# Second attention: features of q by head, on 64-row halves of the partitions, and scores in one pass

## The chip, the cores and the metric

The kernel runs on one core of one Trainium2 chip. The metric is the device time of one execution in microseconds (us), as the median of several executions. A profile of one further execution goes with it: its span, its engines (PE for matmuls, PEld for the loading of weights, DVE, ACT, POOL, and SP, which only issues DMAs here), and every instruction with its start and duration.

## What is computed

The program is two layers on an input of 4 batches of 512 tokens by 128 features. Each layer normalises x, computes an attention s and a gated mixture of experts g, and adds s * silu(g) to x. The change concerns the attention of the second layer, 16 heads of 8 dimensions, repeated over 16 "wavelength" channels:

```
Q, K, V = x Wq + bq, x Wk + bk, x Wv + bv     # per head: [512, 8]
for each channel w:   m = cos(phase[w, head])
    scores = (Q m)(K m)^T / sqrt(8);  scores *= cos(KERR scores^2)
    acc += softmax(scores) V * interference_weight[w]
out = (acc / 16) Wo + bo
```

With the data's sizes the inner cosine is 1, and the channel only scales the scores by a number a between 0 and 1. The kernel therefore does not compute 16 softmaxes. It writes exp(a s) as a sum of six functions of s: exp(A s), its square and its cube, and s squared, s and 1. The first three ("bank 0") need the scores of all pairs of query and key; the last three ("bank 1") need only sums over the keys of products of the components of k and v, and then a product with features of q. A numerator and a denominator of each channel are then mixtures of the banks. If the data were outside the assumed sizes, a second, general version of the program would run after it; it does not run here.

## The kernel before

The last stage of the program, `attn1`, is a loop of 64 steps i = 0 to 63: for each of the 4 batches b, 16 steps t = 0 to 15; step t works on the group m = t // 4 of four heads and on the block t % 4 of 128 keys. Instructions that go through the helpers `mm1` (L318), `act1` (L321), `vec1`, `pool1` and `dma1` (L330) keep the order in which they are written, on each engine, so the order within a step is the order of the text.

A step issues, on PE, the scores of the *next* step (`scores1`; the page calls the tile `s`), then the sums over keys of *this* step (`over_keys`; tile `acc`). ACT computes exp(A s) of the next step and then its square, in two halves of 128x1024 each (`function1`), and DVE the cube as the product of the two (L1548). `acc` of a step takes the three functions one after the other; the cube comes last. Every fourth step begins a new group of heads: there DVE first copies `acc` away (L1590, tile `bank`), and the next `acc` has to wait for that copy.

The scores are exact to about 24 bits although they are bf16 matmuls: q and k are split into three bf16 parts each (`partq`, `partk`), and 8 products of parts per dimension are summed. A head has 8 dimensions times 8 products, 64 rows. Before the change these lie as two sets x = 0, 1 of 32 rows; four heads stand beside each other on the 128 partitions; `scores1` (L1525) runs two passes of four matmuls of 32 rows, the second of which adds to the first.

Bank 1 of group m is two matmuls in `bank1` (L1328), one of 65 rows (`rows1`: 32 components of q of four heads, their squares, a row of ones) and one of 128 rows (`rows2`: the products of component d with component d + 1 to d + 4 of the same head, cyclically). Their weights `lin` come from `forms` (L1272): sums over the 4 blocks of 128 tokens of products of `feat` (the same features of k, made on POOL at L1203 to L1218) with v; only the diagonal blocks, where the head of the feature is the head of v, are kept by the multiplication with `count` (L1286, L1290). `features1` (L1312) fetches the rows of q from DRAM by 6 DMAs per group (`qe`, `qd`) into `rows1`, `rows2` and a buffer `other`, and POOL multiplies (L1324, L1325).

Extra work is placed on the steps by hand. `mixing` (L1593) gives the steps at which `bank1`, `sums1` (denominators), `quotients1` and `output1` run, and `prepare1` (L1168) spreads the preparation of the next batch over steps 0 to 15 by a table (tokens 0, 1 and 13, projections 2 and 3, `forms` 5, 7, 10 and 11). At steps with t % 4 = 0 this extra PE work stands ahead of `acc`, at the others behind it. The preparation of batch 0 runs between the experts of the stage before (`prepare`). PSUM tiles with the tag "mix", two buffers, are shared by `bank1`, `sums1`, `quotients1` and `output1`. `end1` finishes the last batch.

## Time and profile before

| | us |
|---|---|
| median of 3 runs (lowest, highest) | 886.55 (886.23, 888.0) |
| profiled execution | 890.56 |
| its span, first to last instruction | 888.8 |
| PE, DVE, ACT, POOL busy in the span | 850.0, 596.3, 520.1, 383.4 |
| loop of the second attention in the span | about 534 to 868 |
| end of the last batch | about 868 to 888.8 |

An fp32 matmul stands in the trace as two matmuls, each with its weight load, so `x4` of the tile `b` is one call of `bank1`. Tiles of matmuls are written rows*columns of the array ("65*128"). Matmuls in different tiles of the array run beside each other, so the busy time of a group is less than the number of its instructions times the duration of one. The chain of waits lists pieces in order of time, each with its start in the span and its length; "issue" is time in which an engine waited for nothing that the profile shows. The profiled execution took 890.56 us, 4.01 us more than the median of the runs.

### The profile page before, as it was taken

To read this page: it belongs to the slowest core of one execution; us is meant where nothing else is said; L and a number is where in the kernel's file an instruction comes from. 1 tells how busy PE (TensorE), PEld (TensorE's weight loads), DVE (VectorE), ACT (ScalarE), POOL (GpSimd) and SP (SyncE) were. 2 spreads that over 40 slices of the span, in tenths; PEclk is the share of its full clock that TensorE was granted. 3 is DMA by queue.
4 is the path that set the end of the run, shared out by engine and by line. 5 is a ranking of instruction groups with operands and counts; after the bars stand their busy time and mean duration, and the time that the engine had idled before them with its cause. 6 is when DMAs were issued, how large, how long until landed. Compare 5 with 4: busy or idle time off the path is not lost. (4 is left out here: it accounts for less than half of the span.)

```text
span 888.8 us, 19127 instructions
## 1 busy us (share of the span) xinstructions
PE 850.0 (96%) x7660; PEld 525.9 (59%) x7660; DVE 596.3 (67%) x1202; ACT 520.1 (59%) x692; POOL 383.4 (43%) x471
## 2 busy tenths in 40 slices
PE   8998899999999999989999998999999999989996
PEld 4565688898888969877677772333234224322324
DVE  7774666667668868863353337687876888677684
ACT  3433565656566665642432249778776787768780
POOL 7840244545444433563033007853934492441112
PEclk9999999999999989999999999999999999999999
DMA  8501421212122121100005002354151324130000
GB/s 213 140 14 39 117 62 43 80 25 84 37 61 72 38 60 37 27 1 1 1 1 178 1 1 72 126 164 110 53 172 53 87 92 128 58 87 30 1 13 15
DMA packets 77055, 57.64 MB, mean 65 GB/s; under 512 B 40176, under 2 KB 65040, under 8 KB 76960
## 3 DMA queue, kind: packets, MB, share of 16 engines
q1 hardware_dynamic: 74768, 54.94, 21.1%
q0 software_dynamic: 1616, 1.16, 0.8%
q8 instruction: 62, 1.02, 0.5%
q10 hardware_dynamic: 576, 0.26, 0.1%
q14 instruction: 33, 0.27, 0.1%
HBM read 35.36 MB, written 20.97 MB: 63 GB/s over the span
## 5 line engine op out<-in xcount | busy, mean ns | idle before, releaser
L1548 DVE TENSOR_TENSOR e<-e,e 128x1024 f32<-128x1024 f32 x126 | 182.2, 1486 | 78.1 <-ACT e L321 78.1
L318 PE MATMUL acc<-e,strip 128*32 128x512 f32 x1520 | 185.0, 601 | 11.8 <-DVE bank L1590 10.4
L321 ACT ACTIVATE e<-s 128x1024 f32<-128x1024 f32 x126 | 122.1, 1022 | 69.0 <-PE s L318 69.0
L321 ACT ACTIVATE e<-e 128x1024 f32<-128x1024 f32 x126 | 126.4, 1060 | 0.0
L318 PEld LDWEIGHTS acc<-e,strip 128*32 128x32 f32 x1520 | 44.9, 110 | 125.5 <-issue 86.6
L321 ACT ACTIVATE h<-ph 128x1024 f32<-128x1024 f32 x32 | 32.8, 1024 | 87.5 <-PE ph L318 87.4
L318 PEld LDWEIGHTS eo<-w_out,h 128*128 128x128 f32 x512 | 62.5, 196 | 11.7 <-issue 10.4
L321 ACT ACTIVATE pj<-pp 128x512 f32<-128x512 f32 x64 | 38.2, 597 | 50.4 <-PE pp L318 50.2
L318 PE MATMUL eo<-w_out,h 128*128 128x128 f32 x512 | 64.5, 281 | 1.0 <-DVE g L971 0.8
L772 POOL TENSOR_TENSOR t<-t,gate 128x512 f32<-128x512 f32 x32 | 40.8, 1276 | 56.9 <-DVE t L705 41.7
L971 DVE SCALAR_TENSOR_TENSOR g<-eo,gw,g 128x128 f32<-128x128 f32 x112 | 31.5, 344 | 48.7 <-PE eo L318 48.7
L318 PE MATMUL dot<-vone,E 128*128 128x65 f32 x512 | 61.1, 273 | 0.0
L318 PEld LDWEIGHTS dot<-vone,E 128*128 128x128 f32 x512 | 59.8, 192 | 1.1 <-issue 0.8
L318 PE MATMUL ph<-xnT,w_in 128*128 128x512 f32 x128 | 60.3, 594 | 0.0
L724 POOL TENSOR_TENSOR t<-t,gate 128x512 f32<-128x512 f32 x32 | 40.9, 1279 | 33.7 <-DVE t L705 33.7
L747 DVE TENSOR_TENSOR mz<-mz,mu 64x512 f32<-64x512 f32 x56 | 38.4, 685 | 19.3 <-PE mu L318 18.7
L667 DVE SCALAR_TENSOR_TENSOR elu<-elu,up 128x512 f32<-128x512 f32 x60 | 42.4, 707 | 7.2 <-ACT up L321 6.4
L773 POOL TENSOR_TENSOR t<-t,t 128x512 f32<-128x512 f32 x32 | 45.7, 1429 | 2.5
L321 ACT ACTIVATE attT<-pa 128x512 f32<-128x512 f32 x32 | 19.1, 597 | 46.2 <-PE pa L783 46.2
L643 DVE TENSOR_TENSOR E<-sc,cap 128x1024 f32<-128x1024 f32 x32 | 39.0, 1220 | 9.6 <-PE sc L318 7.0
L740 POOL TENSOR_TENSOR mz<-mz,zs 64x8 f32<-64x8 f32 x56 | 11.7, 209 | 70.3 <-DVE zs L672 61.6
L321 ACT ACTIVATE E<-E 128x1024 f32<-128x1024 f32 x32 | 33.6, 1051 | 11.5 <-DVE E L643 11.5
(279 smaller groups left out, 1629.4 us busy)
## 6 DMA issues: line engine op xcount, KB each, us to landing
vd<-vt SPq DMA_DIRECT2D x32, 256.0 KB
vone<-vd SPq DMA_DIRECT2D x64, 128.0 KB
k<-kd SPq DMA_DIRECT2D x16, 256.0 KB
q<-qd SPq DMA_DIRECT2D x16, 256.0 KB
rows<-qd SPq DMA_DIRECT2D x64, 64.0 KB
other<-qe SPq DMA_DIRECT2D x16, 256.0 KB
kd<-partk SPq DMA_DIRECT2D x12, 256.0 KB
qd<-partq SPq DMA_DIRECT2D x12, 256.0 KB
```

The source lines that it names most:

```text
L318: return self.pin(self.nc.tensor.matmul(*args, **kw))
L321: return self.pin(self.nc.scalar.activation(*args, **kw))
L643: self.vec1(nc.vector.tensor_tensor(e.rearrange("p x hp c -> p (x hp) c"), ps.rearrange("p x hp c -> p (x hp) c"), bc(self.cap.rearrange(" ...
L667: self.vec1(nc.vector.scalar_tensor_tensor(t, t, 1.0, up, ALU.min, ALU.add))
L724: nc.gpsimd.tensor_mul(t, t, self.gate)
L740: nc.gpsimd.tensor_add(new[half, :, :, p, DK].rearrange("d hp a -> d (hp a)"), old[half, :, :, p, DK].rearrange("d hp a -> d (hp a)"), seg ...
L747: self.vec1(nc.vector.tensor_tensor(new[half, :, :, p, 0:DK], old[half, :, :, p, 0:DK], ps[half, :, :, p * 64 : p * 64 + 64].rearrange("d ...
L772: nc.gpsimd.tensor_mul(t, t, gate2)
L773: nc.gpsimd.tensor_add(t, t, seg[n]["t1"])
L971: self.vec1(v.scalar_tensor_tensor(acc[b][:, k, :], eo[:, k, :], w, acc[b][:, k, :], ALU.mult, ALU.add))
L1548: self.vec1(self.nc.vector.tensor_mul(t, src[0][pair], src[1][pair]))
```

## The change

Each head of the second attention gets its own 49 rows of features of q: 5 blocks of 8 products (component d with component d + 0 to d + 4, `SHIFTS`), 8 plain components, and a row of ones. Two heads with the same place r in the groups 2mm and 2mm + 1 stand on partitions 0 to 48 and 64 to 112 (`HALF`).

- `bank1` works on two groups at once: 8 matmuls of 64 rows by 32 columns, each of which fills the 32 output partitions of one head. It is called at steps 8 and 15 instead of 4, 8, 12 and 15, takes both "mix" buffers, and its two results go to SBUF by two evictions in the following step.
- `forms(mm, first)` computes the weights head by head: 16 matmuls, 49 columns of weights and 9 moving columns each, in two column tiles of 64, instead of 8 with 65 or 128 columns and 36 moving columns. The diagonal blocks are computed alone. Two DVE multiplications follow instead of four.
- `feat` is made by five multiplications and a copy, and the squares of k are a part of it; the separate square (L1203) and the copies L1208 and L1212 go for k.
- `features1` loads two groups by four DMAs with rows of 8 KB into `rows1[mm]` and a common `other1`; POOL multiplies each head's 128x512 block, 8 a batch. Loads and multiplications have fixed steps (`loads`, `makes`): for mm = 0 of batch b loaded at step 9 of the batch before and multiplied at its steps 12 and 13, for mm = 1 loaded at step 1 and multiplied at steps 6 and 7; batch 0 begins at steps 1 and 4. q goes to DRAM once, doubled, by 8 DMAs of 64 KB instead of 3 of 256 KB.
- The parts of q and k lie in DRAM so that the 64 rows of a head are 64 partitions; `scores1` is one pass of four matmuls of 64 rows, without accumulation.
- `opening1` places the first step's functions in `rows1[0]` and `rows1[1]`. `count` is made of 3 columns by selections on POOL. Nothing else changes.

The lines taken out are in the functions above; here most of them are left out.

```diff
--- before.py
+++ after.py
-ROWS1 = 65
+SHIFTS = 5
+LINEAR = SHIFTS * D1
+ROWS1 = LINEAR + D1 + 1
+HALF = 64
...
-        self.feat = keep.tile([P, 16, ROWS1 + P], F32, name="feat")
-        nc.gpsimd.memset(self.feat[:, :, ROWS1 - 1 : ROWS1], 1.0)
+        self.feat = keep.tile([P, 4, H1, ROWS1], F32, name="feat")
+        nc.gpsimd.memset(self.feat[:, :, :, ROWS1 - 1 : ROWS1], 1.0)
...
-            lin = keep.tile([P, 2, 4, 4, 32], F32, name=f"lin{k}")
+            lin = keep.tile([P, 2, 4, 32], F32, name=f"lin{k}")
...
-        self.rows1 = keep.tile([P, 4, S], F32, name="rows1")
-        self.rows2 = keep.tile([P, 4, S], F32, name="rows2")
+        self.rows1 = [keep.tile([P, 4, S], F32, name=f"rows{mm}") for mm in range(2)]
+        self.other1 = keep.tile([P, 4, S], F32, name="other")
+        nc.gpsimd.memset(self.other1, 1.0)
...
+                feat = self.feat.rearrange("p k h r -> p (k h) r")
                 self.pool1(nc.gpsimd.tensor_copy(twice[:, :, D1 : 2 * D1], t))
...
+                for d in range(SHIFTS):
                     self.pool1(nc.gpsimd.tensor_mul(
...
+                        feat[:, :, d * D1 : (d + 1) * D1], t, twice[:, :, d : d + D1]
                     ))
+                self.pool1(nc.gpsimd.tensor_copy(feat[:, :, LINEAR : LINEAR + D1], t))
+                now["squares" + w] = feat[:, :, 0:D1]
...
-                    once = now["once"] = self.a1d.tile([P, S], F32, name=f"qe{b}", tag="qe")
-                    self.dma1(once, t)
                     twice = now["twice"] = self.a1d.tile(
-                        [H1, 2 * D1, S], F32, name=f"qd{b}", tag="qd"
-                    )
-                    for k in range(2):
-                        self.dma1(twice[:, k * D1 : (k + 1) * D1, :], t)
+                        [4, 2 * D1, 4, S], F32, name=f"qe{b}", tag="qe"
+                    )
+                    for m in range(4):
+                        for k in range(2):
+                            self.dma1(
+                                twice[m, k * D1 : (k + 1) * D1].rearrange("d r s -> r d s"),
+                                t[m * 32 : m * 32 + 32],
+                            )
                 dram = now["parts" + w] = self.a1d.tile(
-                    [2, P, 4, S], BF16, name=f"{w}d{b}", tag=f"{w}d"
+                    [P, 2, 4, S], BF16, name=f"{w}d{b}", tag=f"{w}d"
                 )
...
-                        self.dma1(dram[x, :, at:end:step], bc(part, 1, n))
+                        self.dma1(dram[:, x, at:end:step], bc(part, 1, n))
...
+        def forms(mm, first):
+            heads = range(first, first + 2)
             def pe():
...
+                ps = psum.tile([P, 2, 9], F32, name=f"pl{b}_{mm}_{first}", tag=tag[0], bufs=tag[1])
+                for r in heads:
                     for k in range(4):
...
+                        for o in range(2):
+                            h = (2 * mm + o) * 4 + r
+                            self.mm1(
+                                ps[o * HALF : o * HALF + ROWS1, r - first],
+                                lhsT=self.feat[:, k, h], rhs=strip[:, k, h, 18:27],
+                                start=(k == 0), stop=(k == 3),
+                            )
                 return ps
             def rest(ps):
...
+                for o in range(2):
+                    rows = slice(o * HALF, o * HALF + ROWS1)
                     self.vec1(nc.vector.tensor_tensor(
...
+                        lin[rows, mm, first : first + 2, 0:27].rearrange(
+                            "p r (x d) -> p r x d", x=3
+                        ),
+                        bc(ps[rows], 2, 3), bc(bc(self.count[rows], 1, 2), 3, 9), ALU.mult,
                     ))
...
             return pe, rest
...
     def operands1(self, b, m):
         nc, now = self.nc, self.now1[b]
         for w in ("k", "q"):
...
+            src = now["parts" + w].rearrange("(m u h d) x i s -> m u (h d x i) s", m=4, u=2, h=2)[m]
             t = self.a1q.tile([P, 2, S], BF16, name=f"{w}_{b}_{m}", tag=f"{w}s", bufs=3)
...
+            self.dma1(t, src.rearrange("u p s -> p u s"))
+            now[w, m] = t
+    def features1(self, b, mm):
+        nc, rows, other = self.nc, self.rows1[mm], self.other1
+        for o in range(2):
+            src, at = self.now1[b]["twice"][2 * mm + o], o * HALF
+            each = src[0:D1].rearrange("d r s -> d (r s)")
+            self.dma1(
+                rows[at : at + LINEAR + D1].rearrange("p r s -> p (r s)"), bc(each, 0, SHIFTS + 1)
+            )
+            (step, _), (one, n) = each.ap
+            windows = bass.AP(
+                tensor=each.tensor, offset=each.offset,
+                ap=[[step, SHIFTS], [step, D1], [one, n]],
+            )
+            self.dma1(other[at : at + LINEAR].rearrange("p r s -> p (r s)"), windows)
+        def products(first):
+            for r in range(first, first + 2):
+                self.pool1(nc.gpsimd.tensor_mul(rows[:, r], rows[:, r], other[:, r]))
+        return [lambda: products(0), lambda: products(2)]
+    def bank1(self, b, mm):
         now, psum = self.now1[b], self.a1p
         def pe():
...
+            out = [
+                psum.tile([P, S], F32, name=f"b1_{b}_{mm}_{o}", tag="mix", bufs=2)
+                for o in range(2)
+            ]
+            for r in range(4):
+                for o in range(2):
+                    rows = slice(o * HALF, (o + 1) * HALF)
+                    self.mm1(
+                        out[o][r * 32 : r * 32 + 32], lhsT=now["lin"][rows, mm, r],
+                        rhs=self.rows1[mm][rows, r], start=True, stop=True,
+                    )
+            return out
+        def evict(out):
+            for o, ps in enumerate(out):
+                t = self.a1.tile([P, S], F32, name=f"bank1_{b}_{mm}_{o}", tag="bank1", bufs=3)
+                self.act1(t, ps, AF.Copy)
+                self.banks1[b, 2 * mm + o, 1] = t
         return pe, (lambda _: None), evict
...
-        for x in range(2):
-            for r in range(4):
-                rows = slice(r * 32, r * 32 + 32)
-                self.mm1(
-                    out[r // 2][:, r % 2],
-                    lhsT=now["k", x, m][rows, k * P : (k + 1) * P],
-                    rhs=now["q", x, m][rows], start=(x == 0), stop=(x == 1),
-                )
+        for r in range(4):
+            rows = slice(r % 2 * HALF, r % 2 * HALF + HALF)
+            self.mm1(
+                out[r // 2][:, r % 2], lhsT=now["k", m][rows, r // 2, k * P : (k + 1) * P],
+                rhs=now["q", m][rows, r // 2], start=True, stop=True,
+            )
...
-        e0 = self.function1(0, 0, self.scores1(0, psum, tag, bufs), self.rows1)
-        self.e1 = e0, self.function1(0, 1, e0, self.rows2)
+        e0 = self.function1(0, 0, self.scores1(0, psum, tag, bufs), self.rows1[0])
+        self.e1 = e0, self.function1(0, 1, e0, self.rows1[1])
...
-                    4: lambda: self.bank1(b, 0), 8: lambda: self.bank1(b, 1),
-                    10: lambda: self.sums1(b, 0), 13: lambda: self.quotients1(b, 0, 0),
-                    12: lambda: self.bank1(b, 2), 14: lambda: self.quotients1(b, 0, 1),
-                    15: lambda: self.bank1(b, 3),
+                    8: lambda: self.bank1(b, 0), 10: lambda: self.sums1(b, 0),
+                    13: lambda: self.quotients1(b, 0, 0), 14: lambda: self.quotients1(b, 0, 1),
+                    15: lambda: self.bank1(b, 1),
...
+            loads, makes = {1: [(0, 0)], 4: [(0, 1)]}, {2: [(0, 0, 0), (0, 0, 1)]}
+            for fb in range(B):
+                if fb:
+                    loads[fb * 16 - 7], loads[fb * 16 + 1] = [(fb, 0)], [(fb, 1)]
+                    makes[fb * 16 - 4], makes[fb * 16 - 3] = [(fb, 0, 0)], [(fb, 0, 1)]
+                makes[fb * 16 + 6], makes[fb * 16 + 7] = [(fb, 1, 0)], [(fb, 1, 1)]
+            waiting, late, prep, products = [], [], {}, {}
...
+                for fb, mm, half in makes.get(i, []):
+                    products[fb, mm][half]()
+                for fb, mm in loads.get(i, []):
+                    if fb == 0:
+                        for at in (ROWS1 - 1, HALF + ROWS1 - 1):
+                            self.dma1(self.rows1[mm][at : at + 1], self.other1[at : at + 1])
+                    products[fb, mm] = self.features1(fb, mm)
...
```

## The prediction

> **What bounds the kernel now.** I read the shares of the engines first, then the stretches of the second attention, then its groups by form, the waits, and last the chain of waits around single steps.
>
> ```profile
> span 888.8 us, 19127 instructions
> PE 850.0 (96%) x7660; PEld 525.9 (59%) x7660; DVE 596.3 (67%) x1202; ACT 520.1 (59%) x692; POOL 383.4 (43%) x471
> ```
>
> PE looks like the bound throughout. By batch (us; busy and count of PE, PEld, DVE, ACT, POOL; clock):
>
> ```profile
> 630.00:715.00 85.00, 81.93 (x664) 29.90 (x666) 63.91 (x71) 61.77 (x68) 44.51 (x35) 1.00 0.30 94
> 802.00:868.00 66.00, 61.73 (x511) 19.02 (x510) 49.06 (x53) 51.30 (x56) 10.81 (x9) 1.00 0.04 13
> ```
>
> The groups by form that the change touches (busy, mean ns | idle before):
>
> ```profile
> L318 PE MATMUL s<-q,k 32*128 32x512 bf16 x512 | 39.0, 379 | 1.3 <-DVE g L971 1.3
> L318 PE MATMUL b<-rows,lin 65*128 65x512 f32 x32 | 18.0, 644 | 1.4 <-POOL rows L1324 1.4
> L318 PE MATMUL pl<-strip,feat 128*128 128x36 f32 x128 | 17.0, 279 | 0.0
> L318 PE MATMUL b<-rows,lin 128*128 128x512 f32 x32 | 16.5, 595 | 1.1 <-POOL rows L1325 1.1
> L318 PE MATMUL pl<-strip,feat 128*65 128x36 f32 x128 | 10.4, 228 | 0.0
> ```
>
> But PE also waits, and ACT waits for PE (us in total, times, longest):
>
> ```profile
> ACT e L321 <- PE s L318: 69.0, 47, 3.5
> PEld acc L318 <- DVE bank L1590: 20.0, 13, 2.8
> PE acc L318 <- DVE bank L1590: 10.4, 9, 2.3
> ```
>
> The chain shows why, here around step 56 (batch 3, t = 8):
>
> ```profile
> 824.33 0.60 PE s L318 x8
> 824.93 0.90 issue
> 825.83 1.97 ACT e L321 x2
> 827.85 0.93 issue
> 828.90 1.18 issue
> 830.08 1.21 DVE e L1548
> 831.29 0.61 DVE bank L1590
> 831.95 2.78 PE acc L318 x24
> ```
>
> From the scores at 824.26 to their `acc` at 831.95 are 7.69 us: scores, two exponentials, two squares, the cube, the copy. PE's own work in that time (`acc` 2.71, twice `s` 0.54, `bank1` 1.92) is shorter, and it idles:
>
> ```profile
> 831.95 0.64 PE L318 MATMUL acc<-e,strip 128*32 128x512 f32 x4 [1.91 <-DVE bank L1590]
> ```
>
> So two limits alternate. At most steps PE's sum decides. At the 16 steps with t % 4 = 0 it is the longer of PE's sum and this chain. Reading the starts of `s` and `acc` in the timeline at every such step, `acc` waited for the copy at nine, as the last line of the waits says: t = 4 in batches 1 to 3 (chain 9.0, 8.0, 7.6 us), t = 8 in 1 to 3 (7.7), t = 12 in 3 (6.8), t = 0 of 2 and 3 (9.4). PE's work decided at t = 12 in batches 0 to 2 (7.20), t = 8 in batch 0 (8.21) and t = 0 of batch 1 (7.10). At t = 4 of batch 0 PE waited for POOL's rows. A microsecond of PE work in front of a waiting `acc` is worth nothing.
>
> [...] 4 column tiles (`acc`) start 7 ns apart and 4 row tiles (`s`) 3 ns apart, so both directions work. [...] weight loads of 65 and 128 columns follow each other after 59 and 112 ns[...]. [...] PE was idle for 2.32 us before 792.6, and `acc` then took 4.44 instead of 2.71 us (the third column from the right is the clock):
>
> ```profile
> 792.00:797.00 5.00, 4.39 (x28) 0.94 (x30) 3.68 (x5) 2.15 (x3) 1.74 (x1) 0.66 0.58 151
> 797.00:802.00 5.00, 5.00 (x44) 1.26 (x40) 1.46 (x2) 3.83 (x4) 0.55 (x1) 1.00 0.26 77
> ```
>
> Gaps of 1.91 and 2.00 us did not do it; another, of 2.24, did (397.6).
>
> **The change part by part.** Gains are positive.
>
> *Bank 1.* Before, 16 calls of 1.92 (start of `b` to the next matmul), 30.7 us. After, 8 calls of 8 tiles in two fp32 passes: an `acc` pass of 4 tiles takes 0.45, eight starts 7 ns apart add 0.03, so 0.96 and 7.7 us in all. The 23.0 us less of PE count only where PE decides:
> - t = 4, batch 0: PE stood from 551.7 until POOL's rows came, `acc` began at 557.04; the copy was done at 555.4. Without `bank1` it starts then: 1.6, and 0.2 for the scores below: 1.8.
> - t = 4, t = 8 in batches 1 to 3, t = 12 in batch 3, t = 0 of 2 and 3: 0, the chain covers it. The cover stays.
> - t = 12, batches 0 to 2: PE falls below the chain of 6.8 - 0.2: 3 x 0.6 = 1.8.
> - t = 8, batch 0: from 8.21 to the chain's 7.45, 0.75. t = 0 of batch 1: 0.4, its chain isn't seen and lies between 6.15 (PE) and 7.10.
> - The end: 0.96 less matmul, but the second eviction (0.60) stands ahead of the denominators: 0.3.
> - Two evictions in one step on ACT, ahead of the next exponential, at t = 9 and t = 0: behind long PE steps this is hidden, but `acc` already waited for the cube in the next step at t = 10 of batch 0 (1.5) and t = 1 of batch 1 (0.5): -1.2.
>
> If 64x32 tiles ran only four beside each other, a call would cost 1.9 (-1.5 us in all); better than eight can't be.
>
> *Scores.* `s` takes two waves 0.22 apart before and after (4 matmuls of 64 rows, two beside each other): PE 0. But the first pair of heads is complete after the first wave, so ACT starts 0.22 earlier. That shortens the chain at the nine waiting steps, 2.0, and the two others named, 0.4.
>
> *Forms.* 8 fp32 matmuls in 16 parts take 1.49 now. After, 32 parts with 49 columns[...]; the two column tiles beside each other give 0.74, one after the other 1.47. Pairs in two tiles are nowhere issued faster than 54 ns a matmul (`pp`), though with long streams; at that pace it is 1.76. I take 1.0. It counts at the four calls between the experts, where PE decides, and at t = 5 and 10 of three batches (t = 7 and 11 lie in front of a chain): 10 x 0.5 = 5.0, from -2.7 to 7.5. DVE saves two operations of 0.18 a call, off the path: 0.
>
> *Features of q and k.* POOL multiplied per batch 4 x 1.40 + 4 x 1.56 = 11.8 us, now 8 x 1.56 = 12.5; for k it loses a square and one copy and gains a product, about 1 us less. POOL is 43% busy. The multiplications move to t = 6, 7, 12, 13; queued behind them are the additions of `pr` (t = 7, 15), which `output1` needs only at t = 9: 6 us of slack. Where POOL runs beside the cube, DVE seems slower (mean 1486 against 1222 ns with POOL idle); moving this costs or saves up to 1.5; I take 0. Loads: 4 DMAs of 320 to 384 KB per two groups, 1.4 MB. The first are issued at about 537 for a use at 574; 256 KB took 7 us (`other`), so even one after the other they have the time. On SP 16 issues stand for 27 of about 0.6 a batch; behind the loads wait the operands, needed 25 us later. The loads at t = 9 wait for the bank at t = 8, which is over; those at t = 4 of batch 0 wait for POOL until about 557 and hold q's write, not needed before t = 9. 0, at worst 2 lost. The doubled bank needs both "mix" buffers at t = 15, a DVE product (0.64) later: inside a waiting row, 0.
>
> *Clock.* With less work ahead of a waiting `acc`, gaps grow: at t = 4 to 2.6 to 3.0 in four batches, and in batch 3 to 2.6 (t = 8), 2.7 (t = 12), 3.3 (t = 0); about 1.7 at the others. [...] four of seven, against one now. Each costs up to 1.7, I take 1.5: -4.5, from +1.7 to -10.
>
> *Sum:* 1.8 + 1.8 + 0.75 + 0.4 + 0.3 - 1.2 + 2.4 + 5.0 = 11.3, less 4.5: 6.8. Against the profiled execution, 890.56 (span 888.8), it gives 883.8. That one was 4.0 slower than the median; I take the difference from the median: **879.8**.
>
> **Rivals.**
> - *PE's sum decides everywhere.* For it: 96% busy. Then 23.0 + 16 x 0.5 = 31 us, 855.6. Against it: the waits for the copy, up to 2.8 us, 9 times of 16. Chance 0.05.
> - *The clock eats it: slower.* Place: `acc` after the waits at t = 4, and in batch 3. Price 1.73 each. With forms at 1.47 the gains are 6.5; from five windows more than now the kernel is slower; with all seven gaps and forms at 1.76, 3.8 - 6 x 1.73 = -6.6: 893; typically 889.5. For it: one gap of 2.3 has done it. [...] Chance 0.17.
> - *It doesn't do what it says:* eight tiles run four by four and the forms at issue pace (1.76). 11.3 - 7.7 - 1.5 - 1.5 (fewer windows) = 0.6: 886.0. Chance 0.13.
>
> **How the numbers follow.** Forecast 0.65, its own range 872 to 884.5. Over all cases 871 to 889 leaves out 2 in 10. 0.2% is 1.8 us, about what a measurement of this kernel can tell from no change. Faster by more: the forecast, the first rival, little of the others: 0.71. Within: 0.12. Slower: the clock: 0.17.
>
> **What would show it.** In the changed profile: `b` in 64x32 tiles at about 0.96 a call; `pl` near 1.0 us a call; ACT's exponentials 0.2 earlier after `s`; `acc` still waiting for `bank` at t = 4 with 2.5 to 3 us of idle PE, at t = 12 now too; a lower clock in some of those places; no wait of `b` for POOL. Wrong: PE without gaps (first rival), waits of `b` for `rows`, or `pl` above 1.5.

## The result, and the profile after

The changed kernel takes **912.91 us** in the median of 4 runs (911.11 to 915.89); the kernel before, run beside it, 887.27 (886.23 to 890.13). The ratio is 1.0287, interval [1.0248, 1.0327]: 2.9% slower. The profiled execution has a span of 912.0 us where before had 888.8.

The head of the page (span; busy time, share and number of instructions of each engine):

```profile
span 912.0 us, 19106 instructions
PE 832.6 (91%) x7724; PEld 511.1 (56%) x7724; DVE 597.1 (65%) x1170; ACT 519.4 (57%) x692; POOL 387.5 (42%) x469
```

PE was relieved by 17.4 us and the span still grew by 23.2. The two stretches of the second attention that the prediction showed, here with the same columns (the granted clock is third from the right):

```profile
630.00:715.00 85.00, 75.67 (x660) 25.48 (x664) 63.05 (x61) 59.02 (x65) 44.19 (x32) 0.94 0.31 91
802.00:868.00 66.00, 57.73 (x436) 16.92 (x434) 43.88 (x42) 48.57 (x55) 18.00 (x12) 0.92 0.16 40
```

PE now has room in both, and the clock has fallen from 1.00 to 0.94 and 0.92. The groups by form (busy, mean ns | idle before):

```profile
L321 PE MATMUL acc<-e,strip 128*32 128x512 f32 x1520 | 197.8, 643 | 36.1 <-DVE bank L1614 35.6 <-DVE e L1572 0.5
...
L321 PE MATMUL s<-q,k 64*128 64x512 bf16 x256 | 40.2, 388 | 20.0 <-DMA q<-qd 18.7
...
L321 PE MATMUL pl<-strip,feat 128*49 128x9 f32 x512 | 14.4, 192 | 0.0
...
L321 PE MATMUL b<-rows,lin 64*32 64x512 f32 x128 | 8.9, 601 | 0.0
```

`b` fell from 34.5 us to 8.9 and `pl` from 27.4 to 14.4: the change does what it says. But `acc`, which nobody touched, rose from 185.0 to 197.8 us (601 to 643 ns a matmul), and `s` has 18.7 us of idle time in front of it, for a load of q. The waits say the same (us in total, times, longest):

```profile
ACT e L324 <- PE s L321: 99.0, 48, 21.0
...
PE acc L321 <- DVE bank L1614: 35.6, 15, 3.7
...
PE s L321 <- DMA q<-qd: 18.7, 1, 18.7
```

`acc` waited for the copy of `bank` 9 times and 10.4 us before, 15 times and 35.6 us now. And one wait is new.

**The new wait.** In the timeline of PE it follows the forms of step 10 of batch 0:

```profile
582.68 0.87 PE L321 MATMUL pl<-strip,feat 128*49 128x9 f32 x32
602.25 1.04 PE L321 MATMUL s<-q,k 64*128 64x512 bf16 x4 [18.70 <-DMA q<-qd]
```

The chain of waits, followed back from there (start, length, what):

```profile
576.50 0.70 SPq L333
...
577.24 16.30 DMA other<-qe
593.54 0.02 issue
593.56 0.58 SPq L333
...
596.77 0.71 SPq L333
597.49 0.05 issue
597.54 4.57 DMA q<-qd
602.11 0.14 issue
602.25 0.62 PE s L321 x2
```

The operands q were loaded late because SP issued them late, at 597.5; and SP was held up by a load of factors (`other`) that took 16.3 us to land. What lies between is in the timeline of SP, whose second number is here the time from the first issue to the end of the last:

```profile
577.24 0.73 SPq L333 DMA_DIRECT2D other<-qe  x1
578.07 16.07 SPq L333 DMA_DIRECT2D qe<-qT  x8
594.24 2.43 SPq L333 DMA_DIRECT2D qd<-partq  x5
596.77 0.71 SPq L333 DMA_DIRECT2D k<-kd  x1
597.54 0.70 SPq L333 DMA_DIRECT2D q<-qd  x1
```

Eight writes of `qe`, 0.6 us each, took 16.07. In the trace SP's 289 DMAs have eight completion semaphores, and the 134 of this stage take them strictly in turn. The last four writes started at 582.03, 586.17, 590.10 and 593.56, each 0.01 to 0.02 us after the last update of the semaphore that it takes, which is that of the DMA eight issues before. These are the four loads of the second pair of groups just ahead of them; the waits are 11.1 us in all (us in total, times, longest):

```profile
SPq L333 <- DMA other<-qe: 6.4, 2, 3.5
SPq L333 <- DMA rows<-qe: 4.7, 2, 3.3
```

And these loads were themselves issued late; POOL's timeline gives the beginning of it:

```profile
548.29 0.64 POOL L1227 COPY feat<-tokk 128x512 f32<-128x512 f32 x1
556.71 6.96 POOL L1345 TENSOR_TENSOR rows<-rows,other 128x512 f32<-128x512 f32 x4 [7.78 <-DMA other<-qe]
563.62 1.60 POOL L1271 CAST partk<-kT 128x512 bf16<-128x512 f32 x1
```

POOL did this work in the order of the text, where the products of rows (at 556.71) stand ahead of `partk` (at 563.62), the first of the parts of k and q for batch 1. The rows, issued from 536.1 to 539.3, landed at 556.7; so `partk` came at 563.6, all its writes and the loads behind them on SP moved with it, and 27 us after the late landing PE stood still.

**The clock.** The record of the granted clock has ten stretches at half speed (0.5) in this stage, from 588.0 on, against one before. PE was busy for 38.2 us of them, which is 19.1 us of work lost, against 1.7. Their starts lie on one grid: the steps from 673.37 to 697.26, to 741.64 and to 786.01 are 7, 13 and 13 times 3.413 us. Eight of the ten follow a gap before `acc`, and ahead of each of the eight PE was idle for 2.41 to 2.89 us between two borders of that grid; where none followed, it was idle for at most 1.77 us between two borders of the loop. The gap of 2.72 us at 648.53 lies across a border (649.48), with 1.77 behind it, and was followed by no half clock; one of 2.52 at 669.91 has 2.48 between two borders and was. One stretch in detail: the times of a wait at step 12 of batch 1 and after it (in the same columns as above), and the line of PE:

```profile
693.00:698.00 5.00, 1.37 (x36) 0.85 (x36) 4.94 (x4) 4.74 (x5) 5.00 (x3) 0.93 0.18 61
698.00:705.00 7.00, 6.93 (x36) 1.41 (x40) 4.32 (x6) 1.02 (x3) 0.43 (x1) 0.56 0.00 0
```

```profile
698.07 2.79 PE L321 MATMUL acc<-e,strip 128*32 128x512 f32 x12 [3.70 <-DVE bank L1614]
```

Twelve matmuls of `acc` take as long here as 24 elsewhere. The prediction's clock term had a gap of about 1.7 us for this step; this one is 3.70, because DVE's cubes were slow. DVE and POOL at that moment:

```profile
693.03 4.27 DVE L1572 TENSOR_TENSOR e<-e,e 128x1024 f32<-128x1024 f32 x2 [1.37 <-ACT e L324]
697.33 0.69 DVE L1614 COPY bank<-acc 128x512 f32<-128x512 f32 x1
```

```profile
691.48 6.95 POOL L1345 TENSOR_TENSOR rows<-rows,other 128x512 f32<-128x512 f32 x4
```

Two cubes took 4.27 us beside POOL's products of rows; in the kernel before, with POOL idle from 680.0, the pair at this step took 2.36 (start 679.93). From scores to `acc` were 8.40 us at this step in batches 1 and 2, where the prediction had 6.6.

### The profile page after: what moved, and what is told of

It reads as the page before. It is cut to its first block, busy times and chain, and to the rows that moved or that the text cites. A ratio compares the mean times of both kernels' runs of the same rounds, so it can differ in the third digit from the quotient of the medians.

```text
span 912.0 us, 19106 instructions
## 1 busy us (share of the span) xinstructions
PE 832.6 (91%) x7724; PEld 511.1 (56%) x7724; DVE 597.1 (65%) x1170; ACT 519.4 (57%) x692; POOL 387.5 (42%) x469
## 5 line engine op out<-in xcount | busy, mean ns | idle before, releaser
L321 PE MATMUL acc<-e,strip 128*32 128x512 f32 x1520 | 197.8, 643 | 36.1 <-DVE bank L1614 35.6
L1345 POOL TENSOR_TENSOR rows<-rows,other 128x512 f32<-128x512 f32 x32 | 53.4, 1699 | 45.7 <-DMA other<-qe 23.6
L324 ACT ACTIVATE pj<-pp 128x512 f32<-128x512 f32 x64 | 38.2, 596 | 52.4 <-PE pp L321 52.4
L321 PEld LDWEIGHTS eo<-w_out,h 128*128 128x128 f32 x512 | 60.9, 192 | 11.7 <-issue 10.4
L321 PE MATMUL s<-q,k 64*128 64x512 bf16 x256 | 40.2, 388 | 20.0 <-DMA q<-qd 18.7
L646 DVE TENSOR_TENSOR E<-sc,cap 128x1024 f32<-128x1024 f32 x32 | 39.1, 1220 | 10.2 <-PE sc L321 7.6
L324 ACT ACTIVATE attT<-pa 128x512 f32<-128x512 f32 x32 | 19.1, 597 | 45.8 <-PE pa L786 45.8
```

The lines of the kernel that those rows point to most:

```text
L321: return self.pin(self.nc.tensor.matmul(*args, **kw))
L324: return self.pin(self.nc.scalar.activation(*args, **kw))
L646: self.vec1(nc.vector.tensor_tensor(e.rearrange("p x hp c -> p (x hp) c"), ps.rearrange("p x hp c -> p (x hp) c"), bc(self.cap.rearrange(" ...
L1345: self.pool1(nc.gpsimd.tensor_mul(rows[:, r], rows[:, r], other[:, r]))
```

## The experiments

Three costs were candidates: **the stall** in batch 0, **the half clock**, and **POOL beside the cube** at step 12. All figures are medians; each ratio is to runs of the kernel before on the same chip (887.97 to 889.77 in the sets of runs, 887.27 beside the change). The sets ran on different chips, so a difference of 1 or 2 us between kernels of different sets is not told from none. The work lost at half clock is read from the one profiled execution of each kernel. A *row* is the time from the scores issued in one step to those issued in the next.

### First set: the order of the loads, and gaps filled

*Another order.* In batch 0 the rows are made behind `partk`, not ahead of it, and the second pair is loaded later.

```
-loads, makes = {1: [(0, 0)], 4: [(0, 1)]}, {2: [(0, 0, 0), (0, 0, 1)]}
+loads, makes = {1: [(0, 0)], 7: [(0, 1)]}, {4: [(0, 0, 0), (0, 0, 1)]}
+makes[11], makes[12] = [(0, 1, 0)], [(0, 1, 1)]
# rows of (1, 0): loaded at step 11 of batch 0, made at 14 and 15 (change: 9, 12, 13)
```

> The changed kernel with other steps for the feature loads of batch 0 (second pair of groups loaded at step 7, behind the last operands, multiplied at 11 and 12; first pair multiplied at step 4) and of the first pair of batch 1 (loaded at step 11, behind the operands of step 10, multiplied at 14 and 15). Queue theory: in the changed kernel the operand q of the last group of batch 0 is issued 30 us late, because it stands on SP behind loads that wait for POOL, and PE stands 18.7 us. Then this order takes away the stall and the half clock after it: about 20 us less, 893 (890 to 897), no wait of s for a DMA over 2 us. Rival: POOL and the DMA rings are behind anyway and the stall returns at batch 1's operands: less than 10 us gained, over 903.

Measured: 901.69, ratio 1.0151 [1.0107, 1.0196]. Eleven us better than the change, nine worse than expected. In this order, and in the two of this set built on it, the load of batch 1's rows into the common buffer `other1` stands ahead of the products of the second two heads of batch 0's second pair: those are multiplied with factors of batch 1, which changes part of the computation. It also costs time: the bank at step 15 of batch 0 waits for that landing.

*Scores repeated.* The scores of the next step are computed four more times ahead of a waiting `acc`, to shorten PE's gap.

```
 waiting = [(pe(), *more) for pe, *more in chunks]
+if nxt and i:
+    self.again1(i + 1, e0)        # AGAIN = 4 times scores1 into the same tiles
```

> The changed kernel, in which the scores of the next step are computed four times more into the same place at the steps with t % 4 = 0, ahead of the waiting acc (1.7 us of bf16 matmuls that change nothing). Clock theory: the half-clock windows after the waits cost PE about 17 us outside the stall; with PE busy in the gaps most of them go, at most 3 remain besides the stall's, and the time falls by 10 to 16, to about 900. Rival: the waits themselves are the cost and the clock follows them without a price, since PE has slack: the time stays within 3 us of the changed kernel's or rises.

Measured: 903.42, 1.0175 [1.0137, 1.0213]. Work lost to the half clock fell from 19.1 to 5.1 us, the time by 9.5, where 10 to 16 were expected. The stall is still there, with 15.8 us, so most of the gain is the clock's: the half clock is a cost by itself; how large was not clear until the control below.

*POOL's products moved.* The first order, and the products of the first pair at steps 14 and 15 in the later batches also.

```
-early = 5 if fb == 1 else 7
+early = 5
```

> As the first of these, and the first pair of groups of batches 2 and 3 is loaded at step 11 and multiplied at 14 and 15 too, away from the cube of step 12. POOL theory: at t = 12 of batches 1 and 2 the two cubes took 4.27 us beside POOL's multiplications against 2.36 before, and the gap of 3.7 us cost two windows at half clock. Then acc at t = 12 begins about 6.7 to 7 us after its scores instead of 8.4, and the time is 4 to 8 below the first one's, about 887. Rival: the cube is late for another reason (one-pass scores, DVE's order): within 2 us of the first one's.

Measured: 894.81, 1.0072 [1.0036, 1.0109], 6.9 us below the first order, as expected; the level is 8 us above the expectation, as there.

*All three.*

> Both together: the moved loads and multiplications of the third kernel and the repeated scores of the second. If the stall (20 us), the clock (12 to 16) and POOL (2 to 4) are the whole of the difference and independent, 874 (870 to 880), which is 1 to 2% faster than the kernel before. If the gains of PE in the change are not there once the stalls are gone, it stays at or above 887.

Measured: 891.23, 1.0039 [1.0001, 1.0077], 17 above the expectation. One half-clock stretch was left. The profile shows a row of batch 0 (step 15) of 12.2 us where 4.3 are usual; its `bank1` waits for POOL, and POOL for the load named above:

```profile
614.88 4.93 POOL L1346 TENSOR_TENSOR rows<-rows,other 128x512 f32<-128x512 f32 x4 [16.33 <-DMA other<-qe]
```

### Second set: the order mended, and one half of the change alone

*Order mended.* Both halves of the second pair's products at step 11, ahead of the load.

```
-makes[11], makes[12] = [(0, 1, 0)], [(0, 1, 1)]
+makes[11] = [(0, 1, 0), (0, 1, 1)]
```

> Schedule of loads and makes as before this kernel, with one error of it mended: all four rows of products of batch 0's second pair are now made at step 11, ahead of the load of batch 1's first rows into the same buffer, where two of the four were made behind it; the repeated scores stay in. Theory (three costs, each separate: the 18.7 us stall, the clock windows, the cube beside POOL at t=12): step 15 of batch 0, 12.2 us in the kernel with the error because its 64x32 bank matmuls waited for that load, falls to about 4.3, and the total to 883 (880 to 886), some 4 us below the kernel before, which is the change's own gain (start 2.1 us earlier, 0.9 us less a bank, shorter chains at t=4) less the repeats' cost. Rival (the 64-row rows of products can't be loaded in time in batch 0 whatever the order): the wait moves to another step of batch 0, and the total stays at 889 to 892.

Measured: 892.29 (15 runs), 1.0031 [1.0009, 1.0054]. The expected 883 was missed. Step 15 of batch 0 fell to 4.26 us, but a row of batch 1 grew to 12.05: the wait moved, as the rival had it, though to another batch than it named. The waits in that stretch:

```profile
POOL rows L1346 <- DMA other<-qe: 15.9, 1, 15.9
ACT e L325 <- PE s L322: 9.8, 2, 7.8
DVE sizeq L1235 <- POOL tsqq L1219: 6.9, 1, 6.9
```

POOL stands 15.9 us for the next load, the sizes of q stand behind it in POOL's order, and DVE's cube behind those.

*The same without the repeats.*

> The same schedule without the repeated scores. Theory: the loop then has its gaps of over 2 us before acc again in each group of four steps, and half-clock windows with them: 4 to 8 us above the kernel with the repeats (887 to 891), so at or just above the kernel before, with 8 to 13 us of work lost in half-clock windows. Rival (the windows came from the stalls that are gone, not from the change's shorter rows): fewer than three windows and within 2 us of the kernel with repeats.

Measured: 896.56, 1.0087 [1.0057, 1.0118]: 4.3 above, with 16.3 us of work lost in nine half-clock stretches. The order of loads and products alone has taken 16.4 us off the change.

*Forms moved.* The second call of `forms` from step 11 to 12, ahead of the waiting `acc`:

```
-10: forms(1, 0), 11: forms(1, 2),
+10: forms(1, 0), 12: forms(1, 2),
```

> The kernel with the mended schedule and the repeats, and the second call of forms for the next batch moved from step 11 to step 12, where it is issued ahead of the waiting acc. Theory (PE sets the pace of the rows between two cubes and idles at the cube): its 0.84 us lies inside PE's wait for bank0 at step 12 and leaves step 11, three batches, so 1.5 to 2.5 us less (881). Rival (ACT or DVE sets those rows): within 0.7 us of the kernel without the move.

Measured: 893.76, 1.0042 [1.0019, 1.0064]. No gain: 1.5 above the kernel without the move, with overlapping intervals. The 1.5 to 2.5 us expected are not there.

*The scores alone.* The kernel before with the 64-row operands and the one-pass scores, nothing else.

```
-for x in range(2):
-    for r in range(4):
-        rows = slice(r * 32, r * 32 + 32)
+for r in range(4):
+    rows = slice(r % 2 * 64, r % 2 * 64 + 64)
```

> The kernel before with one part of the change alone: the operands of the scores laid out 64 rows to a head, scores in four matmuls instead of eight; features, rows of products and banks as before. Theory: no new stall, since the loads of the rows of products are the old ones; the chains to acc at t=4 grow shorter as in the whole change, s takes 0.54 us a step where it took 0.54 for eight in two passes, so 0 to 3 us less than before (886), unless the shorter rows open gaps of over 2 us and windows at half clock, each 1 to 2 us: the range is 884 to 893. Rival (the scores are what costs): 8 us or more above the kernel before.

Measured: 886.9 (22 runs), **0.9975 [0.9957, 0.9994]**: 2.3 us faster than before. The prediction had 2.4 for this half of the change; the interval allows 0.5 to 3.8.

### Third set: why does the stall not go away by order?

*One more order.* The rows of batch 1 made at steps 17 and 18, behind all that the loop needs.

```
+at = 17 if fb == 1 else fb * 16 - early + 3
+makes[at], makes[at + 1] = [(fb, 0, 0)], [(fb, 0, 1)]
+loads[fb * 16 + (3 if fb == 1 else 1)] = [(fb, 1)]
```

> The mended schedule with the repeated scores, and batch 1's first rows of products made at steps 17 and 18 instead of 14 and 15, with the load of its second pair at 19 instead of 17. Theory (the stall only moved: POOL takes its work in program order, stood 15.9 us at those products until their load landed at 614.2, and the sizes of q behind them kept DVE's cube waiting, so that one row of batch 1 took 12.05 us for 6.5): nothing that the loop needs stands behind the products any more, that row falls to 6.5 to 7.5, and the median by 4 to 6 us, to 886 to 889 where the kernel before gives 889. Rival (the load's late landing itself holds the loop, whoever waits for it): the 5 us appear again at another row of batch 1, total within 2 us of 892.

Measured: 890.11 (20 runs), 1.0018 [0.9999, 1.0037]. The row at 12.05 fell to 6.26 as the theory said, and the row of step 9 of batch 1, with `po`, rose to 17.2: `partq` waited 8.4 us for the writes of `kd`, which stood behind the later load, and `po` 6.7 for the additions of POOL behind that. The stall had moved a third time, as the rival said, and the total is just inside its range.

*Loads cut in two by heads.* The change's own order, but each load in two DMAs: first the two heads that are multiplied first.

```
-for o in range(2):
-    each = src[0:D1].rearrange("d r s -> d (r s)")
+for r in (0, 2):
+    for o in range(2):
+        each = src[0:D1, r : r + 2].rearrange("d r s -> d (r s)")
```

> The changed kernel with one edit: each load of rows of products and of their factors is cut in two by heads (first the two heads of the first multiplications, then the others), so that its packets have 4 KB and not 8 KB; bytes, places and order of all else as in the change. Theory (the stall comes from when the loads land, and they land late because 8 KB packets end up on few of the DMA engines: 17.5 us for 1.4 MB): the first heads' data land 6 to 10 us after issue, POOL starts to multiply 6 us or more earlier than 556.7, partk and all behind it follow, and the PE stall of 18.7 us shrinks by 6 to 12, the total to 900 to 907. Rival (the order on POOL and SP alone, or the number of DMAs outstanding, sets it): landing at the same time or later, the four DMAs more cost SP 3 us, stall 18 to 22 us, total 912 to 916.

Measured: 898.88, 1.0137 [1.0101, 1.0172], **14.0 us below the change**. The wait for q is 0.8 us instead of 18.7:

```profile
PE s L321 <- DMA q<-qd: 0.8, 1, 0.8
```

POOL no longer waits for the first rows (the change had 7.78 us here); it goes on from the features of k without a pause:

```profile
549.83 0.65 POOL L1227 COPY feat<-tokk 128x512 f32<-128x512 f32 x1
550.43 7.92 POOL L1348 TENSOR_TENSOR rows<-rows,other 128x512 f32<-128x512 f32 x4
```

The DMA packets in the trace tell how the data came. In the change, from 537.7 to 550.5 about 12 packets of 8 KB began per us, six and later five under way at once; then for 5 us only two at once. With loads cut in two, about 26 packets of 4 KB began per us for 13.3 us, also six and later five at once, and no tail followed. The stretches of both kernels (DMA share of 16 engines and GB/s at the end):

```profile
545.00:550.00 5.00, 5.00 (x35) 1.30 (x34) 3.37 (x3) 4.54 (x6) 3.93 (x3) 1.00 0.34 120
550.00:557.00 7.00, 5.24 (x50) 1.37 (x52) 4.28 (x5) 6.05 (x8) 0.29 (x1) 1.00 0.17 48
```

```profile
545.00:550.00 5.00, 5.00 (x38) 1.19 (x30) 3.65 (x3) 4.47 (x6) 5.00 (x4) 1.00 0.70 194
550.00:557.00 7.00, 3.10 (x18) 0.81 (x18) 6.50 (x4) 5.70 (x7) 7.00 (x5) 0.83 0.16 59
```

The first is the change: 0.34 of 16 is 5.4 engines, and in the last 7 us 0.17, 2.7 engines. The second, with cut loads, moves its bytes earlier; its 0.70 at 545 holds the operands k and q beside the rows. Cutting the loads also has a price: POOL's products now run beside the cubes of step 4 of batch 0, which took 4.50 us instead of 2.36. The gap before that `acc` is 3.9 us instead of 1.8, and the first quarter of batch 0 takes 20.5 us instead of 18.4.

*The banks and rows alone.* The change with the two-pass scores and 32-row operands of before.

> The changed kernel with the scores put back as before (eight matmuls of 32 rows in two passes, operands laid out 32 rows to a head): rows of products on half the partitions, their loads, and the 64x32 banks stay. Theory (the cost is in the loads and products of the rows, the one-pass scores are worth 0 to 3 us to the good): 911 to 917, with the stall of 17 to 20 us in batch 0 and six or more half-clock windows. Rival (the one-pass scores share in the loss: by shortening the chains they open the gaps that halve the clock, or their operands' loads come later): 903 to 909.

Measured: 911.7, 1.0246 [1.02, 1.0292]; 19.0 us of work lost at half clock. The loss is all in this half of the change.

*Control: repeated scores in the kernel before.*

> The kernel before with the scores repeated four times ahead of acc at every fourth step, as a control for what the repeats themselves cost: it lost 1.7 us in one half-clock window, so there is little to win back. Theory (the repeats lie inside PE's wait for bank0, and cost next to nothing where the wait is over 2 us): 887 to 891, within 2 us of before. Rival (the repeats delay acc or the operations behind by their own length at some of 15 places): 893 to 899, and then the clock's part in the change was larger than the repeats won back.

Measured: 916.54, 1.0321 [1.0286, 1.0356], 28 us slower, more than even the rival said. The exponential reads the tile that the repeats write, and waits for the last of them (ACT, batch 1):

```profile
628.22 1.94 ACT L322 ACTIVATE e<-s 128x1024 f32<-128x1024 f32 x2 [2.87 <-PE s L319]
```

There are 15 such places, so the mean price is 28 / 15 = 1.9 us. So the 9.5 us that the repeats won in the change were a net gain, and understate what the half clock costs.

### Fourth set: two by two, with matmuls that nothing waits for

Two edits on top of the cut loads: the first pair's rows moved (as in the first set), and six bf16 matmuls of 128x128 at each fourth step into a PSUM tile that nobody reads, ahead of what waits for `bank`.

```
+def fill1(self, i):
+    ps = self.a1p.tile([P, S], F32, name=f"fill{i}", tag="mix", bufs=2)
+    for _ in range(6):
+        self.mm1(ps, lhsT=now["k", m][:, 0, k * P : (k + 1) * P], rhs=now["q", m][:, 0], ...)
```

> The changed kernel with loads cut in two by heads (4 KB packets), and in batches 1 to 3 the first pair's rows of products loaded at step 11 of the batch before and made at steps 14 and 15, where the change has 9, 12 and 13. Theory (two costs are left after the split, POOL beside DVE's cube at step 12 and the half clock; this takes the first): acc of step 12 starts 6.5 to 7.2 us after its scores where it took 8.4, the gap there falls from 3.7 to 2.5 us or less, and the total by 4 to 7 us, to 892 to 895. Rival (POOL's work costs the same wherever it is put): the 7 us of multiplications slow the cubes of steps 0 and 1 instead, total 897 to 900.

> That kernel with one more edit: at each fourth step, ahead of what waits for bank0, TensorE does six 128x128 matmuls of the operands of the scores into a bank of PSUM that nobody reads (1.3 us, work added that changes no output). Unlike the repeated scores, no exponential waits for them. Theory (what is left above the kernel before is the clock alone): no gap before acc is left over 2 us, zero to two half-clock windows instead of six, 0 to 4 us lost instead of 14, and the total falls by 8 to 12 us, to 880 to 885, below the kernel before (889). Rival (the half-clock windows fall in time that the loop waits out anyway, so that they cost little): within 3 us of the kernel without the matmuls.

> Loads cut in two and the six unread matmuls, without the moved loads and products. Theory: costs add, so it stands above the kernel with both edits by what the move is worth without the clock (3 cubes beside POOL at 1.2 to 1.9 us, 3 to 5 us), 884 to 890; the gap of 3.7 us at step 12 shrinks to about 2.4, so one or two windows may stay. Rival (the move's worth was the clock's): within 1.5 us of the kernel with both.

| loads cut in two, and | us | ratio to before | work lost at half clock, us |
|---|---|---|---|
| nothing more | 898.88 | 1.0137 [1.0101, 1.0172] | 14.1 |
| products moved | 896.46 | 1.0088 [1.0061, 1.0116] | 18.3 |
| gaps filled | 886.84 | 0.9968 [0.9951, 0.9985] | 6.7 |
| both | 886.31 | **0.996 [0.9943, 0.9976]** | 1.7 |

Filling the gaps is worth 12.0 us, or 10.2 with the products moved. The profiled executions agree with the clock as the cause: without the move 895.04 and 886.43 us (8.6 less, 7.4 less lost), with it 896.19 and 881.14 (15.0 less, 16.6 less lost). But that last one is the fastest of its 22 executions, at a mean granted clock of 0.996 where their median is 0.9905; the slowest took 891.11 at 0.986. Its 1.7 is a best case.

The move alone is worth 2.4 us and beside the fill 0.5; the intervals overlap in both pairs. In the profiles the quarter (four steps) of batch 1 or 2 that ends with the first `acc` of step 12 takes 23.9 us without the move and 22.0 with it, filled or not. Without the fill it is lost again where the rival of the move looked for it: the quarters that end at step 0 of batches 1 and 3 grew from 20.8 to 23.6 and from 22.1 to 23.6 us. With both edits PE's wait at step 12 of batch 1 looks like this, where the change had 3.70:

```profile
676.79 1.24 PE L322 MATMUL fill<-q,k 128*128 128x512 bf16 x5 [0.16 <-issue]
678.43 2.78 PE L322 MATMUL acc<-e,strip 128*32 128x512 f32 x24 [0.39 <-DVE bank L1628]
```

The two filled kernels are now a little faster than the kernel before, by 0.3 and 0.4%, and the best is the changed kernel with three edits.

### Fifth set: what would the filling do elsewhere?

The same six matmuls in the kernel before:

> Control: the kernel before with the six unread matmuls of 1.3 us at each fourth step and nothing else (work added, outputs unchanged). Theory (the matmuls are worth what the half clock takes, and before lost 1.7 us to it): within 2 us of before (887 to 890), so that the gain of the changed kernel with split loads and matmuls over before is the change's own. Rival (the matmuls are worth 2 us or more in any kernel of this loop): 884 to 886, and the change itself is then worth nothing.

Measured: 895.54, 1.0059 [1.0036, 1.0083]: 6.8 us slower, which neither the theory nor the rival had. There the filling stands in front of a bank of two fp32 matmuls, and together they are longer than the wait; at step 12 of batch 1 `acc` starts 3.99 us into its row instead of 2.46.

And with the scores in one pass alone:

> The kernel before with the one-pass scores alone and the six unread matmuls. Theory (the scores alone lost 3.4 us at half clock, and their gain of 2 us does not need the banks): 883 to 887. Rival (no windows to win back): within 1 us of the scores alone (886.9). Beside it the split and filled change at 886.3: if this one is at or under that, the half-partition rows and 64x32 banks bring nothing of their own.

Measured: 892.5, 1.0045 [1.0027, 1.0064], 5.6 above the scores alone, against both expectations; its profile lost 3.3 us at half clock, the scores alone 3.4. So the filling is no gift to any kernel: in these runs it pays only where the change has emptied the place in front of `acc`. But the scores alone, 886.9, are within 0.6 of the best kernel (ratios 0.9975 and 0.996 on two chips, with overlapping intervals); over them the rows and banks bring nothing that these runs can tell.

### Last: packet size or number of engines?

In the change six and later five packets of these loads were under way at once; the rows repeat 8 partitions six times from one place, the factors are five windows of 8. To test whether the number under way set the time, the loads were cut by partitions, with packets still of 8 KB:

```
-self.dma1(rows[at : at + LINEAR + D1]..., bc(each, 0, SHIFTS + 1))
-self.dma1(other[at : at + LINEAR]..., windows)
+for x in range(0, SHIFTS + 1, 2):
+    self.dma1(rows[at + x * D1 : at + (x + 2) * D1], src)
+for x in range(SHIFTS):
+    self.dma1(other[at + x * D1 : at + (x + 1) * D1], src[x : x + D1])
```

> The changed kernel with its loads cut by partitions instead of by heads: rows of products in three DMAs of 16 partitions each from the doubled tensor qe, the factors in five DMAs of 8, 16 DMAs for a pair where the change has 4; packets stay at 8 KB, bytes, places and order of all else as in the change. Theory ([...] in the change's loads six and five packets are under way at once, from 538 to 551): three of the 16-row DMAs keep up to 16 engines busy and the others 8; the data land by about 550 to 552, little after SP has issued them (16 x 0.7 us), where the change has 556.7; PE's stall of 18.7 us shrinks by 10 or more, to a total of 897 to 905. Rival (8 KB packets as such are slow to land): landing stays at 556 or later, stall 17 to 22, total 910 to 918.

Measured: 908.85, 1.022 [1.0206, 1.0234], 4 us below the change and short of the 897 to 905 expected. The trace has up to 16 packets at once at first and 8 later, as expected, but each takes 833 ns in the mean where it took 467. About 12 packets began per us, no more than in the change with six and five under way. The data need 15.2 us where the change, with its tail, needed 17.9. More packets at once brought no more packets per us in this run. The test is not clean: with 16 DMAs for a pair the last load was issued 10.1 us after the first, and in the change 2.4. The wait for q stays:

```profile
PE s L321 <- DMA q<-qd: 17.9, 1, 17.9
```

So what the cut by heads changes is that the first two heads' rows are there when POOL comes to them, at 550.4, and that its small packets leave no tail. Which of the two does more, and why the last 5 us of the change's loads had only two packets at once, was not separated. Nor was it tried whether SP would go on with more than eight semaphores.

## Why the prediction was wrong, point by point

The forecast was 879.8 us, with 0.71 for faster. The measured 912.9 is outside the range and on the other side.

- **Bank 1: the duration right.** 0.96 us a call was forecast, an estimate from the 0.45 us of an `acc` pass and starts 7 ns apart, as the trace of before has no tile of 64x32; 1.02 was measured (`b` at step 15, first tile to the next matmul). The eight tiles do run beside each other: 601 ns a matmul, and the second pass of eight starts 0.45 us after the first. The first quarter of batch 0, with the wait of t = 4 that was to go, fell from 21.4 to 18.4 us, and `b` waits for POOL's rows nowhere.
- **Scores: right.** 2.4 us forecast for the chain; the scores alone measure 2.3, with an interval of 0.5 to 3.8. In the whole change, putting them back moved the time by 1.2, less than its interval.
- **Forms: right direction, a little better.** 0.84 us a call for 1.0, with 1.49 before. Weight loads of 49 columns come in pairs, one in each column tile, 7 ns apart, and a pair every 46 ns: 16 pairs make the 0.74 us of the prediction, and 1.47 would be 32 loads at that pace one after the other. The loop started at 533.6 instead of 535.7 in the profile; but among the profiles of the other kernels, old forms or new, this start lies anywhere from 529.7 to 535.4, so one pair does not show the gain.
- **The loads: the step that failed.** "The first are issued at about 537 for a use at 574 ... even one after the other they have the time", and of what stands behind them "behind the loads wait the operands, needed 25 us later ... at worst 2 lost". The loads had the time: `b` did not wait. But the use that counts is not PE's at 574. It is POOL's product, 12 us after the issue, and in POOL's queue `partk` stands behind it. Then SP stands behind `partk` and behind the second loads, and the operands of batch 0 behind SP. And four of SP's own issues waited 11.1 us for the landing of the DMA eight before, a wait that the prediction's 0.6 us an issue leaves out. Measured in place of 0 to 2: 18.7 us of PE waiting, 14.0 us of the total when the loads are cut.
- **The clock: the right place, mis-sized.** The term was -4.5: four of seven gaps, 1.5 each; that about half of the gaps would count was the author's estimate. The changed profile has eleven gaps of over 2 us before `acc`, since PE's sum fell below the chain at nearly every fourth step, and of nine gaps of 2.4 to 3.7 eight were followed by a half-clock stretch (the prediction's "window"), not half of them; two of these lasted 6.83 us, twice the usual 3.41. 19.1 us of work was lost against 1.7. By the filled kernels the cost was 10 to 12 us. The slower rival ("the clock eats it", 0.17) named this place, and capped it at seven gaps and 893.
- **POOL beside the cube: taken as 0.** "moving this costs or saves up to 1.5; I take 0". The four products of 6.95 us were put on steps 12 and 13, where the cube's end decides when `acc` starts. Each of two batches had 1.8 us more in the chain; the gaps of 3.7 us are these. This fed the clock rather than the sum: once the gaps were filled, moving the products was worth 0.5.

The durations of PE's work were nearly all right; what they are worth in time is shown for the scores alone. The prediction's sum before its clock term was 11.3. An estimate from two profiles, one execution each: from the first `acc` of the loop to the end, the kernel before took 353.2 us with 1.7 of work lost at half clock, the change with cut loads 357.4 with 14.1. If each us lost is a us of time, that is 8.2 less than before without the half clock. As time measured, the best kernel is 3.0 below the kernel before; 6.8 was forecast. In the order in which they were made, the edits took off 14.0 (cut loads), 12.0 (filled gaps) and 0.5 us (moved products), on chips that are not the same.

The criteria for "wrong" named waits of `b` for `rows`. The wait came at `s`, for q, several in-order waits further on.

## What to carry to other kernels

Where a load feeds an engine that works in program order, the time it has is up to its first reader in that queue, not up to the engine that finally needs the result; list what stands behind that reader, and behind the next queue in turn, and look in the trace for how many DMAs the issuing queue lets out before it waits (here eight). When work is taken from in front of a wait, PE's idle gaps grow, and here gaps of 2.4 us and more mostly cost a stretch at half clock (eight of nine in the change), which took the gain back and more; either use the gain where PE decides, or put work there that nothing waits for, and check by a control that it is hidden. When a stall moves from place to place with every new order, look at the transfer too: here a better order alone took off 16.4 us (896.6) and loads cut in two alone 14.0 (898.9).

## What the runs showed of the hardware

- Rows repeated from one small place in DRAM arrived at 80 to 110 GB/s whether five, six, eight or sixteen packets were under way: 1.44 MB in 17.9 us in the change, in 15.2 cut by partitions, in 13.3 cut by heads. A packet of 8 KB took 467 ns, 833 with more at once; one of 4 KB 205.
- In the loop of the change PE's gaps of 2.47 to 3.24 us before `acc` were each followed by one stretch of 3.41 us at a granted clock of 0.5, except one of 2.72 that was not; those of 3.69 and 3.70 us by one of 6.83; those of 1.76 to 2.12 us by none. The length of the gap alone does not decide: with cut loads gaps of 2.46 to 2.86 us were followed by none four times, and with the products moved too, gaps of 1.78 and 1.79 us by one three times. In the traces of before and of the change all stretches start within 0.1 us of one grid of 3.413 us.
- Two cubes of 128x1024 took 4.27 and 4.50 us beside POOL's products of 128x512 and 2.36 without.
- Within one kernel the executions differ by the clock: the 22 of the best kernel go from 881.14 us at a mean granted clock of 0.996 to 891.11 at 0.986.
- Eight issues of 64 KB writes behind loads that had not landed took 16.07 us on SP, 11.1 of it waiting for the DMA eight before; behind loads cut in two 9.4.
